# Three products of 12-bit parts in place of seven products of matrix halves, in the projections q, v and g of blocks 2 to 7

## The chip, the cores and the metric

The kernel runs on one core of one Trainium2 chip. The core has five engines with queues of their own: PE (matrix products), DVE (vector work), ACT (activations and copies), POOL (a second, slower vector engine) and SP, which here only issues DMAs. An engine takes its instructions strictly in order, so an instruction that waits holds up all that stand behind it.

The metric is the device time of one execution in microseconds (us), as the median of several runs. A profile is one execution of its own, taken with the hardware profiler. Its span, from the first to the last instruction, is a little shorter than the time of a run.

## The reference

```python
# x: (4, 1024, 512) float32; Wq, Wv, Wo, Wg: (512, 512) float32
x = x + _layernorm(_L0_attn_ref(_layernorm(x), ...))
x = x + _layernorm(_L0_ffn_ref(_layernorm(x), ...))

# _L0_attn_ref
q = (x @ Wq.T).reshape(Bsz, Ls, NHEAD, HEAD_DIM)
v = (x @ Wv.T).reshape(Bsz, Ls, NHEAD, HEAD_DIM)
ret = _retention_scan(v, lam)          # state = lam * state + v_t, along the tokens
out = (q * ret).reshape(Bsz, Ls, D)
out = _layernorm(out, ln_gamma, ln_beta)
g = jax.nn.silu(x @ Wg.T)
return (out * g) @ Wo.T

# _L0_ffn_ref: weights rounded to float8_e4m3, products in float32
gate = jax.nn.silu((x @ gate_w) * gate_scale)
up = (x @ up_w) * up_scale
return ((gate * up) @ down_w) * down_scale
```

Four square products of 512 x 512 (q, v, g, o) and a gated FFN of 512 x 1536 x 512, for 4096 tokens.

## The kernel before

**Blocks and steps.** The tokens are cut into eight blocks of 512 (`t`, lines 1051 on). While block t goes through its FFN in 12 steps (`i`), the next block (`b`) goes through its projections, retention, normalization and output product, and for the one after it (`n`) the input is normalized and turned. All of this is one hand-written order: `pe`, `dve`, `act`, `pool` and `sp` keep each engine's instructions in the order of the code. Each FFN step has eight matmuls for gate (bank `pfg`), eight for up (`pfu`) and eight for down (`pd`, two steps late). Between these groups PE does work for the other blocks.

**FFN.** Activations are split into an upper part and a rest in float32r, a type for which each matmul is written as one instruction; the weights are rounded to few bits already. So each FFN product is two float32r matmuls. `pfg` and `pfu` share two banks (`ps_f`): the next gate needs the bank that ACT's silu of the last gate has read, the next up the bank that DVE's multiplication by the last up (the group `gate<-pfu,us_sb,gate`) has read.

**Square products of blocks 2 to 7.** A float32 matmul is written as two instructions. To need fewer, each 512 x 512 x 512 product is done as seven products of halves instead of eight (a Strassen-Winograd scheme): `product` (line 481) does one, with four matmuls of 256 columns, and DVE and ACT add the seven results together through `mids` (`take`, line 570, hands the finished quarters on: v to the scan, q to the multiplication by the retention, g to silu). The sums of halves that it multiplies are made ahead: those of the weights once, in block 0's steps 8 to 10 (`weight_sums`, line 344, on DVE), and stored in DRAM (`keep_sums`, line 375); those of the input per block (`input_sums`, line 465, four subtractions on POOL into `t_sums`). Products read their weights from `w_ring`, four slots of 256 KB, each refilled by SP after the product that read it (`fetch_weights`, line 384).

**Change of block.** In step 9 x rows 0 and 1 of block b, in steps 10 and 11 rows 2 and 3, get their moments (`st`, `mv`: bn_stats on DVE, power on POOL), are normalized (`x1n`), turned (`xs`/`mxs` by way of DRAM for the first two, `pt` on PE for the last two) and split into `x1nT` by ACT and DVE. The gate matmuls of the next block's step 0 read `x1nT`. In the same steps POOL makes the input sums of block n, and PE does n's first three products of v.

**Block 0.** During block 0's FFN, block 1 is projected with plain float32 matmuls from the whole weights. The FFN weights are rounded during the first steps (`scr`), and in steps 8 to 10 the tiles of wv, wq and wg are turned into sums in place and become `w_ring`, `t_sums` and `mids` from step 9 on.

Of the kernel before, what the change touches and what calls it, by code (L numbers as in the profile page):

```python
# [23 lines left out]
def retention_ffn_sandwich(  # L24
# [286 lines left out]
    def turn_by_blocks(dst, src, tag, name):  # L311
# [21 lines left out]
    order = [("v", j) for j in (1, 2, 6, 7, 4, 5, 3)]  # L333
    order += [("q", j) for j in (1, 6, 2, 7, 4, 5, 3)]
    order += [("g", j) for j in (1, 2, 6, 7, 4, 5, 3)]
    order += [("o", j) for j in (1, 2, 6, 5, 3, 7, 4)]
    banks = {
        "v": {1: 0, 6: 1, 5: 0}, "q": {1: 1, 6: 0, 5: 1},
        "g": {1: 0, 6: 0, 5: 1}, "o": {1: 0, 6: 1, 5: 0},
    }  # L340
    squares = {"v": (wvT, wv_sb), "q": (wqT, wq_sb)}
    operands = {}

    def weight_sums():


        for k, (src, w) in squares.items():
            v = src.rearrange("(c p) f -> p c f", p=P)
            a11, a12, a21, a22 = (w[:, i : i + 2, o : o + H] for o in (0, H) for i in (0, 2))
            operands[k] = {1: v[:, 0:2, 0:H], 2: v[:, 2:4, 0:H], 4: v[:, 2:4, H:D]}  # L350
            made[k] = {5: a22, 7: a21, 6: a11, 3: a12}
            dve.tensor_tensor(a22, a21, a22, ALU.add)
            yield
            dve.tensor_tensor(a21, a11, a21, ALU.subtract)
            yield
            dve.tensor_tensor(a11, a22, a11, ALU.subtract)
            yield
            dve.tensor_tensor(a12, a12, a11, ALU.subtract)
            yield

    made = {}
    adding = weight_sums()

    def output_sums():

        v = woT.rearrange("(c p) f -> p c f", p=P)
        b11, b12, b21, b22 = (wo_sb[:, i : i + 2, o : o + H] for i in (0, 2) for o in (0, H))
        operands["o"] = {1: v[:, 0:2, 0:H], 2: v[:, 2:4, 0:H], 3: v[:, 2:4, H:D]}
        made["o"] = {5: b11, 7: b12, 6: b22, 4: b21}
        dve.tensor_tensor(b11, b12, b11, ALU.subtract)  # L370
        dve.tensor_tensor(b12, b22, b12, ALU.subtract)
        dve.tensor_tensor(b22, b22, b11, ALU.subtract)
        dve.tensor_tensor(b21, b21, b22, ALU.subtract)

    def keep_sums(k):
        for j, t in made[k].items():
            operands[k][j] = dram.tile([P, 2, H], F32, tag=f"sum_{k}{j}", name=f"dsum_{k}{j}", bufs=1)
            sp.dma_start(operands[k][j], t)

    RING = 4  # L380
    total_products = len(order) * (NB - FAST)
    fetched = [0]

    def fetch_weights():
        n = fetched[0]
        if n < total_products:
            k, j = order[n % len(order)]
            sp.dma_start(w_ring[:, n % RING], operands[k][j])
            fetched[0] += 1

    class Retention:


        def __init__(self, t, xt=None):
# [7 lines left out]
            self.made = 0  # L402

# [10 lines left out]
        def new_xnT(self):  # L414
            self.xnT = big.tile([P, TB // Q, NC, Q], F32, tag="xnT", name=f"xnT_{self.t}")
            self.by_chunk = self.xnT.rearrange("p g c j -> p c g j")
# [40 lines left out]
        def fetch_x(self):  # L457
            for a in range(NQ):
                sp.dma_start(
                    self.xnT[ts(a, Q)].rearrange("p g c j -> p g (c j)"),  # L460
# [4 lines left out]
        def input_sums(self, *which, engine=pool):  # L465
            x = self.by_chunk
            b11, b12, b21, b22 = (
                x[:, i : i + 2, g : g + TB // Q // 2, :] for i in (0, 2) for g in (0, TB // Q // 2)
            )
            ts_ = [t_sums[:, k].rearrange("p c (g j) -> p c g j", j=Q) for k in range(4)]  # L470
            self.right = {1: b11, 2: b21, 3: b22, 5: ts_[0], 6: ts_[1], 7: ts_[2], 4: ts_[3]}
            ops = {1: (ts_[0], b12, b11), 2: (ts_[1], b22, ts_[0]), 3: (ts_[2], b22, b12), 4: (ts_[3], b21, ts_[1])}
            for k in which:
                dst, x, y = ops[k]
                engine.tensor_tensor(dst, x, y, ALU.subtract)

        def products(self, n=1):
            for _ in range(n):
                self.product()

        def product(self):

            k, j = order[self.made]
            n = (self.t - FAST) * len(order) + self.made
            self.made += 1
            w = w_ring[:, n % RING]
            if j in (1, 6, 5):
                bank = ps_tile(f"p{k}{j}_{self.t}", f"pa{banks[k][j]}").rearrange("p (c f) -> p c f", c=2)
# [5 lines left out]
            for o in range(2):  # L494
                out_ = bank[:, o]
                if k != "o" and len(self.right[j].shape) == 4:
                    out_ = out_.rearrange("p (g j) -> p g j", j=Q)
                for c in range(2):
                    if k == "o":
                        left, right = self.left[j][:, c, ts(o, P)], w[:, c, :]  # L500
                    else:
                        left, right = w[:, c, ts(o, P)], self.right[j][:, c]
                    pe.matmul(
                        out_, left, right,
# [4 lines left out]
            if k == "o":  # L509
                return self.add_o(j, bank)  # L510
            c12, p1, s167 = (mids[:, m] for m in (1, 2, 3))
# [890 lines left out]
```

## Time and profile before

| what | value |
|---|---|
| runs | 969.64, 970.71, 970.82 us; median 970.71 |
| profiled execution, span | 968.2 us |
| granted TensorE clock | 0.997 |
| DMA | 119.04 MB, mean 123 GB/s |
| float32r matmul, 128x512, gate | 768, mean 400 ns |
| float32 instruction, 128x256, `pq<-t_sums,w_ring` | 192, mean 379 ns |
| two-input operation, DVE, 128x512, `wq_sb<-wq_sb` | mean 684 ns |
| the same on POOL, `x<-x,x1n` | mean 1296 ns |
| waits of PE for others, all named | 5.8 us, the longest 1.9 in two waits for DVE's x1n |

Matmuls are pipelined and their ends are modelled, so the mean of one is longer than the distance of two starts; the rate is read from the starts. Line 74 is that of the helper that keeps the order, so almost every instruction carries it, and groups are told apart by the tiles: `pfu<-x1nT,up_sb` writes `pfu` and reads the other two. A time is counted from the start of the span.

### The profile page before, as it was taken

To read this page: it belongs to the slowest core of one execution; us is meant where nothing else is said; L and a number is where in the kernel's file an instruction comes from. 1 tells how busy PE (TensorE), PEld (TensorE's weight loads), DVE (VectorE), ACT (ScalarE), POOL (GpSimd) and SP (SyncE) were. 2 spreads that over 40 slices of the span, in tenths; PEclk is the share of its full clock that TensorE was granted. 3 is DMA by queue.
4 is the path that set the end of the run, shared out by engine and by line. 5 is a ranking of instruction groups with operands and counts; after the bars stand their busy time and mean duration, and the time that the engine had idled before them with its cause. 6 is when DMAs were issued, how large, how long until landed. Compare 5 with 4: busy or idle time off the path is not lost.

```text
span 968.2 us, 11802 instructions
## 1 busy us (share of the span) xinstructions
PE 955.3 (99%) x4118; PEld 764.9 (79%) x4118; DVE 677.9 (70%) x1038; ACT 406.1 (42%) x637; POOL 283.2 (29%) x356
## 2 busy tenths in 40 slices
PE   9999999999999999999999999999999999999997
PEld 7455767778888888888888888888888888888885
DVE  5996999676768578575685766867667675747445
ACT  3555674468656135331433315332153421524223
POOL 1405121402327042250522415242142512314020
PEclk9999999999999999999999999999999999999998
DMA  9311423762436336463236523364242632314021
GB/s 297 128 53 57 152 66 96 221 217 86 142 97 180 126 91 214 127 191 95 97 109 175 161 80 126 103 171 146 77 152 87 184 121 77 109 44 131 0 88 44
DMA packets 96060, 119.04 MB, mean 123 GB/s; under 512 B 8320, under 2 KB 58240, under 8 KB 96000
## 3 DMA queue, kind: packets, MB, share of 16 engines
q1 hardware_dynamic: 95136, 117.62, 39.6%
q8 instruction: 33, 0.54, 0.2%
q10 hardware_dynamic: 864, 0.66, 0.2%
q14 instruction: 27, 0.22, 0.1%
HBM read 86.00 MB, written 32.24 MB: 122 GB/s over the span
## 4 chain that ended last, share of the span: by engine, by line
PE 87%; DVE 6%; DMA 2%; ACT 2%; POOL 1%; issue 1%; SPq 0%; DVEq 0%; ACTq 0%; POOLq 0%
PE pfg L74 16%; PE pfu L74 16%; PE pd L74 15%; PE pq L74 10%; PE pv L74 10%; PE pg L74 9%; PE po L74 8%; DVE scr L74 1%; DVE st L74 1%; DVE y L74 1%; PE pt L74 1%; DMA xnT<-mx 1%; ACT x1n L74 1%; DVE gate L74 1%; POOL mv L74 1%
## 5 line engine op out<-in xcount | busy, mean ns | idle before, releaser
L74 PE MATMUL pfu<-x1nT,up_sb 128*128 128x512 f32 x768 | 205.1, 409 | 0.0
L74 PE MATMUL pfg<-x1nT,gate_sb 128*128 128x512 f32 x768 | 198.1, 400 | 0.1
L74 PE MATMUL pd<-down_sb,fuse 128*128 128x512 f32 x720 | 189.4, 405 | 0.0
L74 PEld LDWEIGHTS pfu<-x1nT,up_sb 128*128 128x128 f32 x768 | 144.5, 188 | 32.1 <-issue 3.1
L74 PEld LDWEIGHTS pfg<-x1nT,gate_sb 128*128 128x128 f32 x768 | 144.2, 188 | 30.3 <-DVE x1nT L74 0.9
L74 PEld LDWEIGHTS pd<-down_sb,fuse 128*128 128x128 f32 x720 | 135.4, 188 | 27.3
L74 ACT ACTIVATE gate<-pfg,gs_sb 128x512 f32<-128x512 f32 x96 | 65.5, 682 | 169.1 <-PE pfg L74 168.9
L74 ACT CAST fuse<-gate 128x512 fp32r<-128x512 f32 x90 | 55.6, 618 | 176.3 <-DVE gate L74 176.2
L74 DVE SCALAR_TENSOR_TENSOR gate<-pfu,us_sb,gate 128x512 f32<-128x512 f32 x96 | 71.8, 748 | 57.9 <-PE pfu L74 56.5
L74 POOL TENSOR_SCALAR mv<-mv 128x1 f32<-128x1 f32 (+1 forms) x82 | 23.5, 286 | 264.0 <-DVE mv L74 260.8
L74 DVE TENSOR_TENSOR fuse<-gate,fuse 128x512 fp32r<-128x512 f32 x90 | 76.8, 853 | 5.5 <-ACT fuse L74 5.5
L74 POOL TENSOR_TENSOR ysum<-y 128x256 f32<-128x256 f32 (+1 forms) x14 | 14.3, 1024 | 195.7 <-DVE y L74 195.7
L74 DVE BATCH_NORM_STATS2 st<-x 128x6 f32<-128x512 f32 x64 | 43.6, 681 | 29.4 <-POOL x L74 26.2
L74 POOL TENSOR_TENSOR mv<-mv,nhalf 128x1 f32<-128x1 f32 (+1 forms) x75 | 48.6, 649 | 6.2
L74 PE MATMUL pv<-t_sums,w_ring 128*128 128x256 f32 x192 | 45.5, 380 | 0.5 <-POOL t_sums L74 0.5
L74 PE MATMUL pg<-t_sums,w_ring 128*128 128x256 f32 x192 | 45.7, 381 | 0.0
L74 PE MATMUL po<-w_ring,t_sums 128*128 128x256 f32 x192 | 45.4, 379 | 0.0
L74 POOL TENSOR_TENSOR x<-x,x1n 128x512 f32<-128x512 f32 x32 | 41.5, 1296 | 13.2 <-ACT x1n L74 12.8
L74 PE MATMUL pq<-t_sums,w_ring 128*128 128x256 f32 x192 | 45.3, 379 | 0.0
L74 PEld LDWEIGHTS pv<-t_sums,w_ring 128*128 128x128 f32 x192 | 36.1, 190 | 6.6 <-POOL t_sums L74 0.7
L74 PEld LDWEIGHTS pg<-t_sums,w_ring 128*128 128x128 f32 x192 | 35.9, 190 | 6.5 <-ACT mids L74 1.3
L74 PEld LDWEIGHTS po<-w_ring,t_sums 128*128 128x128 f32 x192 | 36.2, 189 | 6.0 <-issue 0.3
(168 smaller groups left out, 1512.5 us busy)
## 6 DMA issues: line engine op xcount, KB each, us to landing
kept<-x SPq DMA_DIRECT2D x32, 256.0 KB, 3.0
x<-kept SPq DMA_DIRECT2D x32, 256.0 KB, 4.1
x<-in_x SPq DMA_DIRECT2D x28, 256.0 KB, 4.3
out<-d SPq DMA_DIRECT2D x27, 256.0 KB, 2.0
xnT<-mx SPq DMA_DIRECT2D x24, 256.0 KB, 4.9
w_ring<-dsum_v SPq DMA_DIRECT2D x24, 256.0 KB, 3.5
w_ring<-dsum_q SPq DMA_DIRECT2D x24, 256.0 KB, 2.6
w_ring<-dsum_g SPq DMA_DIRECT2D x24, 256.0 KB, 2.6
```

What stands on the lines that cost most here:

```text
L74: return lambda *args, **kwargs: tc.keep_in_program_order(op(*args, **kwargs))
```

## The change

In blocks 2 to 7, q, v and g are no longer made of seven products. The input and each weight are split exactly into an upper part of 12 mantissa bits, made by masking off the low 12 bits (`top`), and the rest (`low`). Three float32r passes over the whole 512 columns then go into one bank:

- `a`: the unsplit input times the unsplit weight, which enter by their upper bits,
- `b`: the rest of the input times the scaled rest of the weight, after which ACT rescales the bank in place (PSUM to PSUM),
- `d`: a difference of the input times a difference of the weight, each made of its upper part and its rest.

`begin` does `a`, `b` and the rescaling for 128 output columns, `end` does `d` and hands the bank to the scan, the multiplication or silu. 36 such passes of four matmuls of 512 columns replace 21 products; a table, `gaps`, places them among the FFN's groups, up to three passes in a gap. The product o stays as it was, seven products, with its quarters stored in a new place.

The weights are split in block 0's steps 8 to 10 (`WeightSplit`): masks and differences on DVE, the subtraction on POOL for v and g and on DVE for q, the scaling on ACT. The whole weights are stored in steps 2, 3 and 7, the rests and differences in steps 8 to 10. The input is split per block: `tops_of` (mask on DVE, subtraction on POOL) and `diffs_of` (DVE) for token quarters 0 and 1 in steps 9 and 10, 2 and 3 in steps 10 and 11; for block 2 all in block 0's step 10 and 11. `low` and `diff` take the buffers of wq and wg, `mids` that of wo.

```diff
-    order = [("v", j) for j in (1, 2, 6, 7, 4, 5, 3)]
-    order += [("q", j) for j in (1, 6, 2, 7, 4, 5, 3)]
-    order += [("g", j) for j in (1, 2, 6, 7, 4, 5, 3)]
...
+    LOW = 2.0**-12
+    LOW_MASK = -4096
+    stream = [(k, c, part) for k in "vqg" for c in range(NC) for part in "abd"]
+    stream += [("o", j, None) for j in order_o]
...
+    class WeightSplit:
+        def top(self, h):
+            dve.tensor_scalar(
+                self.tops[h].bitcast(I32), self.half(h).bitcast(I32), LOW_MASK, None, ALU.bitwise_and
+            )
+            self.engine.tensor_tensor(self.half(h), self.half(h), self.tops[h], ALU.subtract)
+        def difference(self, h):
+            dve.scalar_tensor_tensor(self.tops[h], self.tops[h], -LOW, self.half(h), ALU.mult, ALU.add)
+            act.activation(self.half(h), self.half(h), AF.Copy, scale=1.0 / LOW)
...
+    gaps = {
+        -2: [("begin", "v", 0)], -1: [("end", "v", 0), ("begin", "v", 1)],
+        0: [("end", "v", 1)], 1: [("begin", "v", 2)], 2: [("end", "v", 2), ("begin", "v", 3)],
+        3: [("end", "v", 3)], 4: [("begin", "q", 0)], 5: [("end", "q", 0), ("begin", "q", 1)],
...
+    }
...
+        def tops_of(self, *which, engine=pool):
+            if which[0] == 0:
+                self.top = big.tile([P, 4, TB], F32, tag="y", name=f"top_{self.t}")
             for k in which:
-                dst, x, y = ops[k]
-                engine.tensor_tensor(dst, x, y, ALU.subtract)
+                x, top = self.quarter(self.xnT.bitcast(F32), k), self.top[:, k]
+                dve.tensor_scalar(top.bitcast(I32), x.bitcast(I32), LOW_MASK, None, ALU.bitwise_and)
+                engine.tensor_tensor(self.quarter(self.low, k), x, top, ALU.subtract)
+
+        def diffs_of(self, *which):
+            for k in which:
+                low = self.quarter(self.low, k).bitcast(F32)
+                dve.scalar_tensor_tensor(
+                    self.quarter(self.diff, k), low, -1.0 / LOW, self.top[:, k], ALU.mult, ALU.add
+                )
+
+        def pass_of(self, bank, k, c, part, start):
+            w = next_unit(k, c, part).rearrange("p (c f) -> p c f", c=NC)
+            x = {"a": self.xnT, "b": self.low, "d": self.diff}[part].rearrange("p g c j -> p c g j")
+            out_ = bank.rearrange("p (g j) -> p g j", j=Q)
+            for i in range(NC):
+                pe.matmul(
+                    out_, w[:, i, :], x[:, i], start=start and i == 0, stop=True, skip_group_check=True,
+                )
+            fetch_weights()
+
+        def begin(self, k, c, home):
+            bank = self.bank[k, c] = ps_tile(f"p{k}{c}_{self.t}", home)
+            self.pass_of(bank, k, c, "a", True)
+            self.pass_of(bank, k, c, "b", False)
+            act.activation(bank, bank, AF.Copy, scale=1.0 + LOW)
+
+        def end(self, k, c):
+            bank = self.bank.pop((k, c))
+            self.pass_of(bank, k, c, "d", False)
...
-            if t == 0 and 8 <= i < 11:
-                for _ in range(4):
-                    next(adding)
+            if t == 0 and i == 8:
+                tops = scratch(2)
+                split_v = WeightSplit("v", wv_sb, tops[0:2])
+                split_q = WeightSplit("q", wq_sb, tops[2:4], dve)
+                split_v.top(0)
+                split_v.top(1)
+            if t == 0 and i in (9, 10):
+                if i == 9:
+                    split_g = WeightSplit("g", wg_sb, [])
+                split_g.tops.append(work.tile([P, PW], F32, tag="xn", name=f"top_g{i - 9}", bufs=1))
+                split_g.top(i - 9)
             f.gate(i)
...
             if n and i == 11:
-                n.input_sums()
-                n.product()
+                n.diffs_of(2, 3)
+                n.gap(-2)
             f.fuse(i)
+            if t == 0 and i == 8:
+                for h in range(2):
+                    split_v.difference(h)
+                    split_v.keep_difference(h)
+                split_v.keep()
+                split_q.top(0)
+                split_q.top(1)
+            if t == 0 and i in (9, 10):
+                split_g.difference(i - 9)
...
             if fast and i == 9:
...
                 if n:
-                    n.input_sums(1, 2)
+                    n.new_parts()
+                    n.tops_of(0, 1)
...
+            if n and t > 0 and i == 10:
+                n.diffs_of(0, 1)
+                n.tops_of(2, 3)
...
+            if t == 0 and i == 8:
+                for h in range(2):
+                    split_q.difference(h)
+                    split_q.keep_difference(h)
+                split_q.keep()
+            if t == 0 and i in (9, 10):
+                split_g.keep_difference(i - 9)
+                if i == 10:
+                    split_g.keep()
...
             if t == 0 and i == 10:
-                t_sums = wpool.tile([P, 4, 2, H], F32, tag="wq_sb", name="t_sums")
-                mids = wpool.tile([P, 4, 2, H], F32, tag="wg_sb", name="mids")
+                n.new_parts()
+                n.tops_of(0, 1, 2, 3)
+                n.diffs_of(0, 1)
```

## The prediction

> **What bounds the kernel now.** I read the page's busy times and chain first, then PE's order of work at one change of block, then POOL and DVE in the same stretch, then ACT, DVE and SP in the last steps of block 0.
>
> ```profile
> PE 955.3 (99%) x4118; PEld 764.9 (79%) x4118; DVE 677.9 (70%) x1038; ACT 406.1 (42%) x637; POOL 283.2 (29%) x356
> PE 87%; DVE 6%; DMA 2%; ACT 2%; POOL 1%; issue 1%; SPq 0%; DVEq 0%; ACTq 0%; POOLq 0%
> ```
>
> PE works through the whole span. Matmul time taken away comes off the end, and every new PE wait is added to it.
>
> ```profile
> 532.31 1.98 PE L74 MATMUL pfu<-x1nT,up_sb 128*128 128x512 f32 x8
> 534.12 1.98 PE L74 MATMUL pd<-down_sb,fuse 128*128 128x512 f32 x8
> ...
> 539.56 1.89 PE L74 MATMUL pv<-xnT,w_ring 128*128 128x256 f32 x8
> 541.10 2.18 PE L74 MATMUL pd<-down_sb,fuse 128*128 128x512 f32 x8
> 543.12 1.03 PE L74 MATMUL pt<-ident,x1n 128*128 128x128 f32 x8
> 543.99 1.89 PE L74 MATMUL pv<-xnT,w_ring 128*128 128x256 f32 x8
> 545.72 1.89 PE L74 MATMUL pv<-t_sums,w_ring 128*128 128x256 f32 x8
> 547.26 2.18 PE L74 MATMUL pfg<-x1nT,gate_sb 128*128 128x512 f32 x8
> ```
>
> Columns: start, length, what, count. Starts give the rates: eight float32r matmuls of 512 columns take 1.815 us (532.31 to 534.12), 227 ns each. A Strassen product is four matmuls, written as eight instructions; between two float32r groups it takes 1.54 us and lengthens the next group from 1.815 to 2.02, so 1.74 together.
>
> ```profile
> 532.29 1.36 POOL L74 TENSOR_TENSOR t_sums<-xnT,t_sums 128x512 f32<-128x512 f32 x1
> 537.67 1.29 POOL L74 TENSOR_TENSOR x<-x,x1n 128x512 f32<-128x512 f32 x1 [0.18 <-ACT x1n L74]
> 539.04 0.19 POOL L74 TENSOR_SCALAR mv<-mv 128x1 f32<-128x1 f32 x1
> 541.10 1.28 POOL L74 TENSOR_TENSOR t_sums<-xnT 128x512 f32<-128x512 f32 x1
> 539.90 0.55 DVE L74 TENSOR_SCALAR x1n<-x,mv 128x512 f32<-128x512 f32 x1
> 540.37 0.74 DVE L74 SCALAR_TENSOR_TENSOR gate<-pfu,us_sb,gate 128x512 f32<-128x512 f32 x1
> 542.58 1.77 DVE L74 TENSOR_TENSOR fuse<-gate,fuse 128x512 fp32r<-128x512 f32 x1
> 545.49 1.27 DVE L74 TENSOR_TENSOR x1nT<-pt,x1nT 128x512 fp32r<-128x512 f32 x2
> ```
>
> The 99% hides how near DVE is here: from 539.90 it has no gap, and its last x1nT ends at 546.76, 0.50 us before the gate matmul that reads it (547.26). POOL does the small mv operations at once and the two late t_sums after them.
>
> ```profile
> 170.95 0.68 ACT L74 ACTIVATE gate<-pfg,gs_sb 128x512 f32<-128x512 f32 x1
> 173.26 2.84 DVE L74 TENSOR_TENSOR wq_sb<-wq_sb 128x512 f32<-128x512 f32 x4
> 177.69 0.72 DVE L74 SCALAR_TENSOR_TENSOR gate<-pfu,us_sb,gate 128x512 f32<-128x512 f32 x1
> 191.77 2.53 SPq L74 DMA_DIRECT2D dsum_g<-wg_sb  x4
> ```
>
> In block 0 the sums of the weights sit between the operations that free the two pf banks (ACT's silu, DVE's gate), and SP stores them. From 158 to 200 DVE is busy 33.1 of 42.0 us and the DMA engines 76%. (Silu n, gate n, up n and fuse n are those of FFN step n.)
>
> **The change part by part.**
>
> *PE's work.* Each of six blocks loses 21 products, 21 x 1.74 = 36.5, and gets 3 squares x 4 columns x 3 passes x 4 = 144 matmuls x 0.2268 = 32.7. Gain 3.8 a block, **22.7** in all. No row has float32r reading xnT's runs of 32. The nearest: float32 reads them (pq<-xnT, 379 ns) as fast as the contiguous t_sums (379), so I take no cost. Ends: 215 ns (half of the 429 pitch of float32 at 512) gives 33; as far the other way, 239, gives 12.
>
> *Lighter DVE, fuller ACT in steps 0 to 6.* Fifteen additions of 0.685 go, eight scans of 0.72 become four of 1.24; ACT gets nine more PSUM passes of 0.59. The shorter DVE buys nothing: it waited for PE there (25.1 us before mids<-pq). The rescaling of a bank lies under the following eight FFN matmuls (1.8 us). With that cover gone it would cost some 0.8 each, 72 times. It is thin in two places. In block 2 the search (1.57+0.19 each, five a step) stands ahead of it on ACT: I find waits of 0.55, 0.35, 0.3, **1.2** in all. Between mean and variance PE now has 3.65 us of units where it had 5.2 of products, and the variance's second half was 0.9 early: 0.25 a block, **1.5** (0 to 5).
>
> *Ring.* 43 loads of 256 KB a block for 28, still four slots. A slot is refilled when its pass ends, and is read again four units on. The tightest case is the second pass of v3: refilled after v2's first pass, it is read after v2's second pass, eight down matmuls, v2's third and v3's first, 0.91 + 1.82 + 0.91 + 0.91 = 4.5 us later; w_ring's groups land in 2.6 to 3.5. I take 0. At the 5.4 that two of them took under stores (issued at 182) it would be 1 us, twice a step, 12 times a block.
>
> *Change of block, five times.* Before, POOL's late t_sums followed the mv of x rows 2 and 3. Now the four subtractions (1.3 each) go in pairs, the second pair ahead of that mv, and DVE gets four masks (about 0.4, half of 0.68 for 128x1024 int32) and four differences (0.75). Walked on this clock: first masks done 533.3, subtractions until 535.7, mv pair 1.7 and the two x additions (ACT between) until 540.5, second subtractions until 543.15, mv, so x1n at 544.15 for 539.90. Queued behind it on DVE: two differences, gate, x1n, fuse, four x1nT, 6.1 us, so 550.3. PE's own way: the v0 second pass starts 543.25, down 544.15, transpose of row 3 at 547.3, the difference pass and v1's first two until 550.45. Without waits PE would be there at 546.8 (7.70 us from 539.56 before; five passes for three products make it 7.24). **3.6 each, 18.** Ends: 2.0 if masks and differences pass beside POOL, 4.5 if each waits out a POOL operation.
>
> That last pair needs a rule. Row: fuse takes 1.77 while POOL subtracts, 0.68 otherwise; no row has a mask or a two-input scalar_tensor_tensor beside a large POOL operation. The Trainium skill ("SBUF — State Buffer", the practical consequences under who interferes with whom) says that a DVE instruction with two SBUF inputs waits out a GpSimd instruction that reads SBUF, whichever came first keeping the port. By it the differences would pay as fuse does, 4.5 a change of block, and the sum below would end at 997; with none waiting it would end at 985.
>
> *Block 0, steps 8 to 11, once.* It gains six masks of 128x1024 (0.68), four POOL subtractions (2.4, twice 1.28 less overhead), two on DVE (1.22), six differences (1.25, by that 1.22), six ACT scalings (1.15), against twelve additions of 0.69. I walk it in the changed program's order; each time is the end of the thing named. First wait: POOL's two v subtractions 170.2 (they start after the mv of x row 0, 165.4), DVE's v differences 172.6, ACT's v scalings and then x1n of row 1 174.85; DVE's q masks, subtractions, the fuse of step 8 and the q differences 180.5; ACT's q scalings 181.7. Only then ACT comes to silu 9, which began at 170.95 before. PE's gate 10 needs the bank that it frees: 182.4 for 175.91. Second wait: the mask of g's second half reuses the buffer of the first, whose four stores stand on SP behind 24 stores of v and q (0.5 to 0.65 each), a turn's stores, its reload and kept of row 2; they land at 197.5. DVE's gate 10 is queued behind that mask, and up 11, which needs its bank, starts at 199. Third wait: DVE's g difference 202, turn and statistics of row 3 203.5, ACT's x1n 205.7, POOL's addition 207.1 and four low subtractions 212.3; the input differences go into wg's buffer and wait until g's last stores have left it, 214.5; then four differences and a bn_stats 218.2. PE: v0's second pass at 212.4, its third 218.3, transpose 219.6, v1's first two until 221.8, and the next gate at 222.2, behind x1nT, for 197.77. With the 0.46 of this stretch already booked as PE gain, **24.9**. Ends: 18 if every overlap goes well; 34 if the stores, 12,288 more packets of 512 B at 41 ns over 16 engines, 31 us, make the DMA engines the limit.
>
> A second rule bears on these waits. Row: the clock is 1.00 from 4 to 960 us and 0.53 from 963 on, PE having stopped at 961.2. The Trainium skill ("TensorE: Matmul & The Clock Gate", the HAM clock gate) says an idle window of 3.4 us halves the clock until a busy one has passed. By it three waits of block 0 would each cost some 1.7 more, 5 us; I leave them out of the sum, since the chain there runs through other engines.
>
> *Sum.* -22.7 + 1.2 + 1.5 + 18 + 24.9 = **+22.9** on the span of 968.2, so 991. The runs' median, 970.71, lies 2.5 above that span: 970.7 + 22.9 = **993**.
>
> **The rivals.** *PE's gain stands alone*: splits and waits hide as the sums did. 970.7 - 22.7 + 2 = 950, faster. For it: PE had waits of 1.6 us in all at these places before. Against it: only 0.5 us of cover at a change of block, and silu 9 behind twelve new operations. It decides if the walks' losses stay under 22.7. *One of the two losses is hidden*: with block 0's gone 970.7 - 22.7 + 18 + 2.7 = 969; with the five changes of block gone 970.7 - 22.7 + 24.9 + 2.7 = 976. For it: each rests on one engine's order. *The ring starves PE*: 12 us a block on top, 993 + 72 = 1065; against it the 4.5 us. *It isn't one pass per matmul*: float32r at the float32 price, 429 for 227, gives 144 x 0.2 x 6 = 175 more; the FFN's rows exclude that nearly.
>
> **How the numbers follow.** Forecast, slower, 0.76; gain alone 0.13; one loss hidden 0.08; the last two 0.03. From the ends, the forecast's own range is 970.7 - 22.7 + 18 + 10 = 976 to 970.7 - 22.7 + 34 + 22.5 + 5 = 1010, of which I keep up to 1008. To leave no more than 2 in 10 out the range takes in the hidden-loss cases: 966 to 1008. This kernel's measurement tells about 0.2% (2 us) from no change. Faster 0.15 (gain alone and a little of the hidden case), same 0.03, slower 0.82.
>
> **What would show it.** Right: new matmuls at 227 ns; PE idle before pfg and pfu in steps 10 and 11 of block 0, released by ACT gate and DVE gate; some 3 us idle at each change of block, released by POOL low or DVE x1n; PE busy share under 97%. Wrong: a pitch over 235, or idle named after w_ring's loads, or no idle at those places, which would make it 950.

## The result, and the profile after

The changed kernel takes **1017.69 us** (median of 4 runs, 1016.39 to 1019.53), the kernel before 970.50 in the same runs: a ratio of 1.0491, 95% interval 1.0476 to 1.0506. It is slower, as forecast, but by 47 us for the 23 forecast, outside the range of 966 to 1008. The profiled execution has a span of 1015.2 us, 47.0 more than before.

The page of the changed kernel, its busy times and its costliest new group (busy time, mean ns of one, then the idle time ahead of it and who ended that):

```profile
PE 958.3 (94%) x3974; PEld 745.3 (73%) x3974; DVE 635.9 (63%) x984; ACT 443.8 (44%) x697; POOL 298.8 (29%) x344
...
PE 66%; DVE 10%; POOL 8%; DMA 5%; issue 5%; ACT 3%; SPq 2%; DVEq 0%; ACTq 0%; POOLq 0%
...
L74 PE MATMUL pv<-low,w_ring 128*128 128x512 f32 x96 | 30.7, 448 | 24.0 <-POOL low L74 24.0
```

PE's list has 144 matmul instructions fewer and is busy for 3.0 us longer, so the gain is not to be seen even in its busy time; and in the chain that ended last PE's share fell from 87% to 66%, the rest of the way now runs through DVE, POOL and DMA. The list of PE's waits (engine, tile, who ended the wait, us in total, times, longest) of the changed kernel:

```profile
PE pv L74 <- POOL low L74: 24.0, 6, 8.4
PE pfg L74 <- ACT gate L74: 8.4, 2, 5.9
PE pfu L74 <- DVE gate L74: 6.4, 1, 6.4
PE pg L74 <- ACT mids L74: 3.7, 6, 0.6
...
PE pv L74 <- DVE total L74: 1.0, 1, 1.0
PE pv L74 <- DMA w_ring<-unit_v3a: 0.6, 1, 0.6
PE pg L74 <- DMA w_ring<-unit_g3b: 0.6, 1, 0.6
```

Before, all waits came to 5.8 us. The first is one wait per change of block, six of them, 8.4 of it in block 0; the second and third are block 0's; the fourth was not foreseen. Measured from one step's first gate matmul to the next one's, the 47.0 us lie here (the forecast split the same way, from its own terms):

| stretch | measured | forecast |
|---|---|---|
| block 0, twelve steps (103.19 before, 134.42 after) | +31.2 | 24.9 - 0.46 = +24.4 |
| step 11 of blocks 1 to 5, the changes of block | +21.4 | 5 x (3.6 - 0.46) = +15.7 |
| all else of blocks 1 to 6 | -6.0 | -22.7 + 6 x 0.46 + 2.7 = -17.2 |
| ahead of block 0, and block 7 | +0.4 | 0 |
| span | +47.0 | +22.9 |

All three are worse than forecast, by 6.8, 5.7 and 11.2. Two of the forecast's own signs came: PE is busy for under 97% (94%) and idles at the places named. So did one of its signs of being wrong, a pitch (distance of two matmul starts) over 235 ns: the new matmuls start 236 to 237 ns apart (experiment 1). First the change of block, PE's order of work in the changed kernel (start, length, what, count, and the wait ahead of it):

```profile
578.50 1.11 PE L74 MATMUL pv<-xnT,w_ring 128*128 128x512 f32 x4
582.60 2.07 PE L74 MATMUL pv<-low,w_ring 128*128 128x512 f32 x4 [2.99 <-POOL low L74]
584.47 2.66 PE L74 MATMUL pd<-down_sb,fuse 128*128 128x512 f32 x8
...
590.68 1.98 PE L74 MATMUL pfg<-x1nT,gate_sb 128*128 128x512 f32 x8
```

The wait stands where the prediction had it. What follows it was not in the forecast: four matmuls take 1.87 (582.60 to 584.47) where the same four elsewhere take 0.95, and eight of down 2.50 for 1.82. The busy times of those stretches (PE, PEld, DVE, ACT, POOL, then the granted clock, DMA share, GB/s) say why:

```profile
582.60:584.50 1.90, 1.90 (x5) 1.51 (x6) 1.01 (x2) 0.00 (x0) 1.57 (x4) 0.50 0.02 6
584.50:586.00 1.50, 1.50 (x5) 1.21 (x4) 1.50 (x4) 0.65 (x2) 0.00 (x0) 0.54 0.12 27
586.00:587.00 1.00, 1.00 (x6) 0.73 (x6) 0.95 (x2) 1.00 (x3) 0.00 (x0) 1.00 0.69 221
```

The clock was 0.50 to 0.54 for 3.4 us after the wait, then 1.00. In block 0, PE of the changed kernel:

```profile
182.16 3.78 PE L74 MATMUL pfg<-x1nT,gate_sb 128*128 128x512 f32 x8 [5.87 <-ACT gate L74]
...
195.89 3.07 PE L74 MATMUL pfg<-x1nT,gate_sb 128*128 128x512 f32 x8 [2.50 <-ACT gate L74]
205.33 3.78 PE L74 MATMUL pfu<-x1nT,up_sb 128*128 128x512 f32 x8 [6.37 <-DVE gate L74]
...
219.09 2.07 PE L74 MATMUL pv<-low,w_ring 128*128 128x512 f32 x4 [8.40 <-POOL low L74]
...
230.23 1.88 PE L74 MATMUL pfg<-x1nT,gate_sb 128*128 128x512 f32 x7 [0.57 <-DVE x1nT L74]
```

Gate 10 starts at 182.16, forecast 182.4. From there on things are late: a wait of 2.5 before gate 11 that was not forecast at all, up 11 at 205.3 for 199, the next block's gate at 229.3 (its later matmuls at 230.2) for 222.2. Who held up ACT and DVE, from their own order of work:

```profile
191.87 0.62 ACT L74 CAST x1nT<-x1n 128x512 fp32r<-128x512 f32 x1 [8.18 <-DMA unit_q3d<-scr]
...
203.92 0.69 DVE L74 TENSOR_SCALAR top_g<-wg_sb 128x1024 int32<-128x1024 int32 x1 [6.36 <-DMA unit_g3d<-top_g]
...
222.40 1.29 DVE L74 SCALAR_TENSOR_TENSOR diff<-low,top 128x512 fp32r<-128x512 f32 x2 [10.08 <-DMA unit_g3b<-wg_sb]
```

All three wait for stores. The second and the third are those of the prediction, which had the third end at 214.5; x row 3's moments stand behind it on DVE, and with them the next block's gate. The first is the surprise: block 1's `x1nT` takes the buffer in which the splits of v and q lay (`scr`), so ACT's cast of row 0 cannot start before the last store of q's differences has left it, and ACT's silu of step 10 is queued behind that cast.

### The profile page after: what moved, and what is told of

Same layout as the page of the kernel before. It is cut to its first block, busy times and chain, and to the rows that moved or that the text cites. A ratio compares the mean times of both kernels' runs of the same rounds, so it can differ in the third digit from the quotient of the medians.

```text
span 1015.2 us, 11825 instructions
## 1 busy us (share of the span) xinstructions
PE 958.3 (94%) x3974; PEld 745.3 (73%) x3974; DVE 635.9 (63%) x984; ACT 443.8 (44%) x697; POOL 298.8 (29%) x344
## 4 chain that ended last, share of the span: by engine, by line
PE 66%; DVE 10%; POOL 8%; DMA 5%; issue 5%; ACT 3%; SPq 2%; DVEq 0%; ACTq 0%; POOLq 0%
PE pd L74 12%; PE pfg L74 12%; PE pfu L74 11%; PE pv L74 9%; PE po L74 8%; PE pq L74 8%; PE pg L74 7%; POOL low L74 2%; SPq L74 2%; DVE st L74 2%; POOL mv L74 2%; DVE scr L74 1%; DVE y L74 1%; DVE gate L74 1%; DVE fuse L74 1%
## 5 line engine op out<-in xcount | busy, mean ns | idle before, releaser
L74 PE MATMUL pfu<-x1nT,up_sb 128*128 128x512 f32 x768 | 198.5, 401 | 6.4 <-DVE gate L74 6.4
L74 POOL TENSOR_SCALAR mv<-mv 128x1 f32<-128x1 f32 (+1 forms) x82 | 27.7, 338 | 264.2 <-DVE mv L74 260.3
L74 DVE TENSOR_TENSOR fuse<-gate,fuse 128x512 fp32r<-128x512 f32 x90 | 78.3, 870 | 10.2 <-ACT fuse L74 10.2
L74 POOL TENSOR_TENSOR ysum<-y 128x512 f32<-128x512 f32 x8 | 11.0, 1369 | 214.3 <-DVE y L74 214.3
L74 POOL TENSOR_TENSOR mv<-mv,nhalf 128x1 f32<-128x1 f32 (+1 forms) x75 | 54.3, 725 | 6.2
L74 PE MATMUL pv<-low,w_ring 128*128 128x512 f32 x96 | 30.7, 448 | 24.0 <-POOL low L74 24.0
L74 DVE TENSOR_TENSOR y<-pq,y 128x512 f32<-128x512 f32 x24 | 16.6, 692 | 54.7 <-PE pq L74 54.7
L74 POOL TENSOR_TENSOR d<-d,x 128x512 f32<-128x512 f32 x28 | 36.0, 1310 | 22.7 <-ACT d L74 20.9
L74 ACT ACTIVATE pv<-pv 128x512 f32<-128x512 f32 x24 | 14.0, 582 | 65.1 <-PE pv L74 65.1
L74 PEld LDWEIGHTS pv<-low,w_ring 128*128 128x128 f32 x96 | 19.3, 207 | 31.2 <-POOL low L74 26.8
L74 DVE RECIPROCAL rstd<-rstd 128x512 f32<-128x512 f32 x8 | 26.8, 3352 | 21.8 <-ACT rstd L74 21.8
```

The costliest lines, as they stand in the source:

```text
L74: return lambda *args, **kwargs: tc.keep_in_program_order(op(*args, **kwargs))
```

## The experiments

Times are medians of four runs; the changed kernel is 1017.69 (1016.39 to 1019.53), and the kernel before, measured again beside the experiments, stayed between 970.5 and 971.3. The runs of one kernel spread over 1 to 5 us.

**1. Reading contiguous columns.** Tokens and channels of the input are mixed up by this edit.

```diff
-            x = {...}[part].rearrange("p g c j -> p c g j")
-            out_ = bank.rearrange("p (g j) -> p g j", j=Q)
+            x = {...}[part].rearrange("p g c j -> p (g c j)")
+            x = x.rearrange("p (c f) -> p c f", c=NC)
+            out_ = bank
```

> Every matmul of q, v and g in blocks 2 to 7 reads 512 columns that lie side by side in place of sixteen runs of 32 (the tokens and channels are mixed up by it, so q, v and g are not those of the reference; count and shape of the matmuls stay). The changed kernel's new matmuls start 236 to 237 ns apart, those of the FFN 227. Theory (the strided reading costs 10 ns a matmul): pitch 227 in all three passes, 864 x 0.0098 = 8.5 us shorter, 1009. Rival (the ring's weights, or the bank that is added to, cost it): pitch stays 237, 1017 to 1018.

**1008.53**, 9.2 less. PE's order of work, first in the changed kernel, then in this one, each between the same three groups:

```profile
595.26 1.11 PE L74 MATMUL pv<-xnT,w_ring 128*128 128x512 f32 x4
596.21 1.11 PE L74 MATMUL pv<-low,w_ring 128*128 128x512 f32 x4
597.15 1.98 PE L74 MATMUL pd<-down_sb,fuse 128*128 128x512 f32 x8
```

```profile
591.55 1.07 PE L74 MATMUL pv<-xnT,w_ring 128*128 128x512 f32 x4
592.46 1.07 PE L74 MATMUL pv<-low,w_ring 128*128 128x512 f32 x4
593.37 1.98 PE L74 MATMUL pd<-down_sb,fuse 128*128 128x512 f32 x8
```

Four matmuls take 0.945 from start to start when each reads sixteen runs of 32, 0.91 when the columns lie side by side: 236 and 227 ns. The length in the second column blurs this (1.11 and 1.07 contain the modelled end); starts show it. The theory holds, and the rival (the ring's weights, or adding to the bank) falls. One thing went with the reading: the bank, which lies side by side in both kernels, is no longer described as sixteen runs of 32. Experiment 7 changes both together too, so no run parts the two. The prediction's count of PE's work comes out once the columns are contiguous: in this kernel block 6, the last one with new matmuls and without a split of the input at its end, is 2.8 us shorter than before, 3.4 without its wait for ACT's mids, where the count gives 3.8 - 0.46 = 3.3.

**2. Work in the wait.**

```diff
-            self.pass_of(bank, k, c, "a", True)
+            again = 0 if (k, c) != ("v", 0) else 8 if self.t == FAST else 3
+            self.pass_of(bank, k, c, "a", True, again)
...
-            for i in range(NC):
+            for i in list(range(NC)) * (1 + again):
```

> v0's first pass is repeated in the wait before its second one: three times more in blocks 3 to 7 (2.8 us of the 3.0 to 3.5 us), eight times more in block 2 (7.6 of 8.4 us); each repetition starts its sum anew, so the result is the same. Theory (the wait makes the clock fall to half, and that costs 0.9 in v0's second pass and 0.7 in the down group after it): both run at 237 and 227 ns, and each change of block is 1.1 to 1.4 shorter, until DVE's last x1nT (589.6 for a gate that starts at 590.7) sets the end; 5.5 to 7 in all, nothing in block 0, where DVE's differences set the next pass: 1011. Rival (the clock falls on its own, whatever PE does): 1017 to 1018, the slow matmuls stay.

**1014.30**, 3.4 less, so more work for PE made the kernel faster. Busy times and clock over v0's second pass and the down group behind it, in this kernel:

```profile
584.60:585.84 1.24, 1.05 (x4) 0.86 (x5) 0.16 (x1) 0.00 (x0) 0.99 (x4) 1.00 0.29 40
585.84:587.70 1.86, 1.86 (x10) 1.49 (x9) 1.86 (x4) 0.58 (x1) 0.72 (x2) 1.00 0.62 175
```

The clock stays at 1.00, the four matmuls take 1.05, the eight 1.83. What step 11 has over the kernel before fell in four of the five changes (5.10 to 3.60, 4.48 to 3.60, 4.56 to 3.59, 3.62 to 2.65) and not in the first (3.62 to 3.68), 4.3 together, under the 5.5 to 7 expected. The exception fits: in the changed kernel PE waited 2.98 to 3.52 us at each change, and after the first wait (3.07) its four matmuls took 1.05, the clock 1.00.

So the length of a wait does not decide: 3.07 left the clock alone and 2.98 halved it. The trace of the changed kernel shows what went with it. Its granted clock changes only at times that lie a whole number of steps of 3.41 us apart. Here are five such stretches and, last, the half-speed one behind the fifth (columns as above; the value behind the comma is PE's busy time):

```profile
193.34:196.75 3.41, 0.91 (x5) 0.73 (x5) 1.10 (x3) 2.37 (x5) 1.28 (x1) 1.00 0.87 227
336.70:340.11 3.41, 1.63 (x8) 0.97 (x6) 1.75 (x4) 3.38 (x5) 3.27 (x4) 1.00 0.31 117
340.12:343.53 3.41, 2.13 (x9) 1.76 (x10) 1.25 (x3) 0.66 (x2) 2.78 (x6) 1.00 0.36 112
459.58:462.99 3.41, 0.50 (x2) 0.45 (x3) 0.88 (x2) 0.17 (x1) 3.24 (x5) 1.00 0.65 217
579.05:582.46 3.41, 0.56 (x3) 0.11 (x1) 1.42 (x4) 0.80 (x2) 3.41 (x3) 1.00 0.62 214
582.46:585.87 3.41, 3.27 (x8) 2.59 (x9) 2.38 (x5) 0.58 (x1) 1.65 (x5) 0.50 0.06 20
```

The first wait (3.07) lies across a boundary: PE is busy for 1.63 and 2.13 of its two stretches, and the clock stays. In the other four changes one stretch holds nearly the whole wait (PE busy for 0.42 to 0.56), and the clock is at one half for the next one. In block 0 a stretch with a wait of only 2.50 (busy 0.91) was enough. All thirteen traces agree: away from their start and end, every such stretch at full clock in which PE was idle for more than 0.55 of the time was followed by half speed, and none with less than 0.37 was. The Trainium skill ("TensorE: Matmul & The Clock Gate", the HAM clock gate) has a window of about 3.4 us that runs freely, and this trace agrees with both; it asks for an idle window, though, where here one that was idle for 2.5 of its 3.4 us was enough.

**3. POOL's late subtractions behind mv.**

```diff
-        -2: [("begin", "v", 0)], -1: [("end", "v", 0), ("begin", "v", 1)],
-        0: [("end", "v", 1)], ...
+        -2: [("first", "v", 0), ("first", "v", 1)], -1: [("second", "v", 0), ("second", "v", 1)],
+        0: [("end", "v", 0), ("end", "v", 1)], ...
             if n and t > 0 and i == 10:
                 n.diffs_of(0, 1)
-                n.tops_of(2, 3)
             if fast and i == 10:
                 b.x1_moments(2)
                 b.x1_moments(3)
                 b.x1n_of(2)
+            if n and t > 0 and i == 10:
+                n.tops_of(2, 3)
```

`first` is the first pass, `second` the second with the rescaling; `n.diffs_of(2, 3)` moves behind the last `rest_of(3)` of step 11.

> At the change of block POOL's subtractions for token quarters 2 and 3 come after the mv of x rows 2 and 3, DVE's differences of these quarters after the four x1nT, and PE does the first passes of v0 and v1 first, both second passes after the transposes, both difference passes after the next gate. Theory (the order on POOL, low ahead of mv, is the whole loss at the change): on the clock of the change at 578 us mv starts at 580.1 for 582.6, x1n of row 3 is ready at 582.0 to 582.6, low at 584.6 under the down group, next gate 586.7 for 590.7, no halved clock: 4 each, 20 in all, 998, and 1 to 3 more in block 0. Rival (DVE's own work, masks and differences, sets it): x1nT comes out at the same time, at most 5 in all, 1012.

**1009.98**, 7.7 less. Step 11 got 16.7 shorter over the five changes; but one pass per change (0.95) has only moved into the next step 0, which the expectation forgot, and step 0 grew by up to 2.1. DVE and POOL at one change of this kernel:

```profile
581.16 2.68 POOL L74 TENSOR_TENSOR low<-xnT,top 128x512 fp32r<-128x512 f32 x2
...
581.70 1.02 DVE L74 TENSOR_SCALAR x1n<-x,mv 128x512 f32<-128x512 f32 x1
582.64 1.75 DVE L74 TENSOR_TENSOR fuse<-gate,fuse 128x512 fp32r<-128x512 f32 x1
584.32 1.28 DVE L74 TENSOR_TENSOR x1nT<-x1n,x1nT 128x512 fp32r<-128x512 f32 x2
```

At this change no wait of PE is over 1 us any more, and the clock stays at 1.00. What is left is DVE: with POOL's subtractions now beside its last operations, x1n takes 1.02 for 0.55 and fuse 1.75 for 0.68. So the order on POOL was about half of the loss. The other half goes with the two engines working beside each other, which experiment 8 takes apart.

**4 and 5. Block 0 in parts.** In the fourth kernel the rests and differences of the weights are made but not stored, in the fifth not made either (`top` and `difference` are empty).

```diff
-            keep_units(self.k, "b", by_unit(self.w))
+            for c in range(NC):
+                operands[self.k, c, "b"] = operands[self.k, c, "a"]
...
-                sp.dma_start(operands[self.k, c, "d"][:, 2 * h : 2 * h + 2, :], d[:, :, ts(c, P)])
+                operands[self.k, c, "d"] = operands[self.k, c, "a"]
```

> The splits of the weights are made, but the rests and differences are not stored: the second and third passes read the unsplit weights (their products are not those of the reference). 36 stores of 512 B packets on SP go. Theory (the stores hold up block 0: the mask of g's second half, up 11 behind it, and x1nT, which takes the buffer of q's differences): the wait of 6.4 us before up 11 and the one of 2.5 before gate 11 go, the input's low starts 8 to 10 earlier: 1006 to 1009. Rival (the splits themselves, on DVE, ACT and POOL, fill the stretch): the waits before gate 10 (5.9) stays in both; here up 11 stays late too, at most 2 gained, 1015.

> The weights are neither split nor stored in parts: second and third passes read the unsplit weights (their products are not those of the reference). Of block 0's additions only the input's masks, subtractions and differences are left. Theory (the splits' operations and their stores make block 0's loss): without the stores alone 12 of 31 us went in the profile; without the operations the wait before gate 10 (5.9) goes too and low of the input, 8 to 10 late in step 11, comes in its turn: block 0 loses 4 to 6, 990 to 993. Rival (what is left, the input's four subtractions on POOL behind the x of row 3, sets the end of step 11 by itself): over 12 stays, 998 or more.

**1002.16** without the stores, 15.5 less; **996.02** without the splits, 21.7 less. In the profiles block 0 loses 19.1 and 8.0 in place of 31.2. By the medians the stores were the larger part and more than expected; by the profiles the two steps weigh about the same, 12.1 and 11.1. The waits before gate 11 and up 11 are gone with them, that before gate 10 (5.9) stays, as both theories had it, and goes in the fifth. What remains without any split, 8.0, lies between the 4 to 6 of the theory and the rival's 12. PE and DVE of the fifth kernel:

```profile
198.74 2.08 PE L74 MATMUL pv<-low,w_ring 128*128 128x512 f32 x4 [8.83 <-POOL low L74]
...
194.16 3.40 DVE L74 SCALAR_TENSOR_TENSOR diff<-low,top 128x512 fp32r<-128x512 f32 x2 [3.10 <-POOL low L74]
```

It is the change of block once more: POOL's four subtractions stand ahead of the mv of x row 3, as the rival had it, though they cost less than it said. The second line also prices what no row of before showed: a difference with two SBUF inputs beside POOL's subtraction takes 1.7 (3.40 for two), alone 0.68.

**6. Silu 9 ahead of the scalings, fewer stores.**

```diff
+            if t == 0 and i == 9:
+                split_q.scale(0)
+                split_q.scale(1)
+                split_q.keep()
```

These lines stand behind `f.gate(9)`; `difference` no longer scales q, and each half of a difference is stored by two DMAs.

> The two ACT scalings of q's rests and their stores come after silu 9 in place of before it, and a difference's half is stored with two DMAs in place of four (24 stores for 36). Theory (order on ACT and the stores cost, not the amount of work): silu 9 at 174.5, the wait before gate 10 falls from 5.9 to under 1; the buffers that wait for stores (x1nT's, that of the mask of g's second half) come free 4 to 6 earlier: 10 to 12 less, 1006 to 1008. Rival (DVE is full from step 8 to 11, 43 us of work in 42, whatever the order): gate 10 is early, but the 6 us come back before up 11 or in step 11: 1014 to 1017.

**1017.26**: nothing gained. PE's wait before gate 10 (5.9) is gone, and 4.4 stand before up 10, 4.3 before gate 11 (2.5 in the changed kernel) and 7.2 before up 11 (6.4). ACT in this kernel:

```profile
190.87 0.62 ACT L74 CAST x1nT<-x1n 128x512 fp32r<-128x512 f32 x1 [7.97 <-DMA unit_qd<-scr]
```

The cast waits as long as before, for the same bytes in half as many DMAs. Its stores of 256 KB in 512 B packets land some 0.9 us apart (v's rests at 183.6, 184.6, 185.5 and 186.4), those of 128 KB in the changed kernel 0.46 apart (q's differences at 190.2, 190.7, 191.2, 191.6): here the bytes ahead in the queue set the time, not the number of issues. The rival is right in its outcome, but not in its reason: DVE idles 5.8 us at that place.

**7. Rests and differences side by side, and g's banks.**

```diff
-            shape = [P, TB // Q, NC, Q]
+            shape = [P, NC, TB]
...
-                elif (k, c) in (("g", 1), ("g", 2)):
-                    self.begin(k, c, "pa0")
+                elif k == "g":
+                    self.begin(k, c, f"pa{(0, 1, 1, 0)[c]}")
...
-            var = ps_tile(f"var_{self.t}", "pa1" if self.fast else "pa")
+            var = ps_tile(f"var_{self.t}", "pa0" if self.fast else "pa")
```

> The rests and differences of the input are made channel chunk by channel chunk and written with 512 tokens side by side, so the second and third passes read contiguous columns and only the first one runs of 32; and g's banks and that of the variance change places (g1, g2 on pa1, g3 and the variance on pa0), so that g1 does not wait for the silu of g0. Theory: pitch 227 in 576 matmuls, 0.0098 x 576 = 5.6 us, and the six waits for ACT's mids (0.6 each, 3.7) go: 9.3 together, 1008. Rival: writing or reading in runs makes POOL's and DVE's operations longer than 1.28 and 0.68, and the change of block gives 5 or more back, 1013 or more; or the wait at g1 comes back at g2 or at the variance, then 1012.

**1007.48**, 10.2 less, 9.3 expected. The six waits for ACT's mids are gone from PE's list; the variance waits 1.4 in all for DVE's half in their place. POOL's subtractions stayed at 1.3 with runs of 32 as their source.

**8. All subtractions of the input in step 9.**

```diff
                 b.x1_moments(0)
                 b.x1_moments(1)
+                if n:
+                    n.new_parts()
+                    n.tops_of(0, 1, 2, 3)
```

> As the run with low after mv, but in blocks 1 to 5 all four masks and subtractions of the input follow the moments of x rows 0 and 1 in step 9, where POOL is idle until 573 on the clock of the change at 577. Theory (x1n of row 3 and the fuse, 1.02 and 1.75 long beside POOL's low, are what was left of the loss): both fall to 0.55 and 0.7, the next gate at 584.9 for 586.35, 1.4 at each of five changes: 7 less than with low after mv, 1003. Rival (the same waits of DVE for POOL only move to step 9 and 10, to its x1n, fuse and moments, and DVE has not enough slack there): no gain over that run, 1010 or more.

**1024.32**, 14 more than experiment 3 and slower than the changed kernel itself. DVE, then PE, of this kernel:

```profile
575.04 3.59 DVE L74 TENSOR_SCALAR top<-xnT 128x512 int32<-128x512 int32 x4 [1.17 <-DMA xnT<-mx]
578.55 0.74 DVE L74 SCALAR_TENSOR_TENSOR gate<-pfu,us_sb,gate 128x512 f32<-128x512 f32 x1
...
579.34 3.15 PE L74 MATMUL pfu<-x1nT,up_sb 128*128 128x512 f32 x8 [2.42 <-DVE gate L74]
```

The masks come to DVE before their data has landed and wait 1.17; four of them then take 3.59, for 1.42 where POOL is idle, since POOL's subtractions run beside the last two (1.5 each, 0.42 for the first two). Queued behind them is the gate operation that frees up 10's bank, and PE waits 2.4 for it; step 10 is 2.9 to 6.6 longer than before the change at the five changes. Step 11 itself got 1.2 shorter than before the change, so the reading of experiment 3 was right and the place was wrong: the rival's outcome.

**9. Only the order of the stores.**

```diff
                     split_v.keep_difference(h)
-                split_v.keep()
...
                 split_g.difference(i - 9)
+                split_g.keep_difference(i - 9)
+                if i == 9:
+                    split_v.keep()
+                    split_q.keep()
```

`split_q.keep()` and g's `keep_difference` leave their old places.

> Only SP's order in block 0's steps 8 and 9 is changed: the stores of the differences of v, q and of g's first half come before those of the rests of v and q, and no longer behind x row 2's copy and the ring's first loads. Same operations, same bytes. Theory (two buffers wait for stores: x1nT takes that of q's differences, whose last store lands at 190.8, and g's second mask that of the first, landing at 203.6): the cast of x1nT row 0 at 188 for 191.9, the wait before gate 11 (2.5) gone; the second mask at 193 to 195 for 203.9, the wait before up 11 (6.4) down to 2 or less; 8 to 10 less, 1008. Rival (the amount of work on DVE, ACT and POOL sets the end of step 11 and the stores only hide behind it): the waits move to POOL's low, 1015 to 1018.

**1010.36**, 7.3 less, block 0 at +25.9. ACT, then PE, of this kernel:

```profile
187.94 0.62 ACT L74 CAST x1nT<-x1n 128x512 fp32r<-128x512 f32 x1 [4.69 <-DMA unit_q3d<-scr]
...
196.48 2.12 PE L74 MATMUL pfu<-x1nT,up_sb 128*128 128x512 f32 x8 [2.21 <-DVE gate L74]
204.08 2.05 PE L74 MATMUL pv<-xnT,w_ring 128*128 128x512 f32 x4 [5.48 <-DMA w_ring<-unit_v0a]
210.30 2.07 PE L74 MATMUL pv<-low,w_ring 128*128 128x512 f32 x4 [4.18 <-POOL low L74]
```

The cast comes at 187.9 (188 expected), gate 11 has no wait, up 11 waits 2.2 for 6.4. The theory holds. It left out a wait of 5.5: the ring takes wv's buffer, so its first load now stands behind v's and q's rests. That wait costs little, since the pass behind it has to wait for POOL's low until 210.3, and POOL's chain to it does not use the ring. What sets the end is the third hand-over: DVE's differences of the input wait 11.6 for the last store of g's rests, until 215.1, for 222.4 in the changed kernel.

**10 and 11. All orders together, and without the splits.** The edits of 3, 6 (ACT), 7 and 9, and in block 0 the input's masks and subtractions behind the moments of x row 3, its differences behind the `x1nT`. The eleventh adds that of experiment 5.

> All reorderings together, exact results: low after mv at every change (in block 0 the input's masks and POOL's subtractions come after the moments of x row 3 too, the differences after the x1nT), rests and differences side by side, g's banks, q's scalings behind silu 9, the order of stores. Theory (the losses are separate and add up): 1017.7 less 7.7 (low after mv), 10.2 (side by side and banks), 8 to 10 (stores and silu 9), 4 to 5 (row 3 in block 0): 985 to 988. Rival (block 0 is full: DVE has 43 us of work in 42 us of steps 8 to 11): block 0 gives under 5, 993 to 1000. Faster than the kernel before (971) by neither.

> As all orders together, but the weights are neither split nor stored in parts (second and third passes read the unsplit weights, the products are not those of the reference): what the three passes are worth in blocks 2 to 7 when block 0 costs nearly nothing. Theory (losses add up): 996.0 less 7.7, 10.2 and 4 to 5 = 973 to 975; against 971 before the gain of PE, 22.7 by my count less 3 for the runs of 32 that are left, is then still eaten by some 20 us of waits at the changes and in step 0 after them. Rival (with block 0 free the passes win): 960 or less.

**986.99** (ratio to before 1.0175, interval 1.0159 to 1.0191) and **975.15** (1.0050, 1.0032 to 1.0068): the first inside what the separate losses add up to, the second at its upper end. PE's waits in the tenth:

```profile
PE pfu L74 <- DVE gate L74: 7.1, 2, 4.4
PE pv L74 <- DMA w_ring<-unit_v0a: 5.5, 1, 5.5
PE pt L74 <- DVE x1n L74: 5.3, 5, 1.3
PE pfg L74 <- DVE x1nT L74: 5.1, 5, 1.0
```

The first two are block 0's, which still loses 16.2 of the 16.9 that this profile is above that of before; the others are DVE's x1n and x1nT at the changes. Two thirds of the loss (30.7 of 47.2) were order and layout. Even with no split of the weights at all (and so with the wrong products), the three passes only come to within half a per cent of the kernel before: no version tried here beats it.

## Why the prediction was right on the side and wrong on the size

Three terms of the sum missed by much: PE's gain was put some 8 us too high, the changes of block 5.7 and block 0 6.8 too low. Smaller terms missed both ways.

**PE's work.** "I take no cost" for reading runs of 32 was the step that cost most. It was argued from a row of another type. The pitch is 236 to 237 ns, almost the upper end of 239 that the prediction had set and did not use. So 144 matmuls take 34.07 us a block and the gain is 36.5 - 34.07 = 2.43, 14.6 in all for 22.7; experiment 1 measured the difference at 9.2. Some 7.3 of it (744 of the 864 matmuls) lie in the third row of the table and make up most of its 11.2; waits for ACT's mids, the ring and a sum of the search (5.9 in all, for 2.7 booked) make up 3.2. The estimate had looked for the cost in a float32 row (379 and 379 ns), where it did not show; there a column takes about twice as long (216 ns for 256 columns, 227 for 512 in float32r).

**The range.** Its upper end was added up with the full 22.7 of gain. With the gain of 12 that belongs to 239 ns, it would have ended at 970.7 - 12 + 34 + 22.5 + 5 = 1020, and held. The bound was worked out and then left out of the sum. It would have held by luck in part: the other ends in it, 4.5 a change of block if the differences waited for POOL, 34 in block 0 if the DMA engines were the limit, 5 for the variance, stand for causes that did not come.

**The lighter DVE, the fuller ACT.** The 1.2 for the search (ACT's passes `seen` over the FFN weights) and 1.5 for the variance did not come where they were put: no wait of PE is named after a rescaling or the variance. One wait of 1.0 belongs to the search in another place, where v's first pass waits for DVE to read the search's last sum (`total`) out of a bank. ACT did cost 3.7, at a place not looked at: g1 begins in the bank that g0's silu still reads, and that silu stands behind the squares and the step's own silu. Experiment 7 took it away by other banks.

**The ring.** 0 was near: two waits of 0.6.

**Change of block.** Place, order and the engine named (POOL's low ahead of mv) were right, and PE waited 2.98 to 3.52 where the walk had about 3. Measured +21.4 for +15.7: 4.3 of the difference is the halved clock (experiment 2), 1.0 the pitch of five passes each. The prediction had the clock's rule before it and applied it to block 0 alone, and there left it out of the sum; as quoted it asks for an idle window of 3.4 us, which a wait of 3 is not, and the stretches under experiment 2 show that less was enough. That DVE's differences would wait out POOL did not happen in this order: they ran at 0.68 beside mv. Where they meet a subtraction they pay 1.7 (experiment 5), as the rule of the Trainium skill quoted there says ("SBUF — State Buffer", the practical consequences under who interferes with whom).

**Block 0.** The walk was exact to its first wait, and in its steps too (POOL's v subtractions 170.5 for 170.2, DVE's q differences 180.4 for 180.5, gate 10 182.16 for 182.4). It then missed the buffer that `x1nT` takes over from the splits, which put 8.2 us of waiting into ACT's queue, and what follows came some 6 to 7 later. Experiment 9 shows that the order of the stores did it: with another order, block 0 is back to +25.9. Its points lie near those of the walk: up 11 at 196.5 for 199, the second pass at 210.3 for 212.4, the differences' wait over at 215.1 for 214.5, the next gate at 223.4 for 222.2. The new order moved the stores that `x1nT` waits for together with those that the second mask waits for, so how much each of the two cost is not shown. The clock, left out of the sum there, was at one half for 30.7 us of this stretch in the changed kernel; no run shows what that cost by itself. This stretch is also the one that varies: the kernels above that leave its splits and stores as they are had 31.2 to 35.1 in their profiles, so a difference of a few us there rests on the medians, and 25.9 lies well outside.

**The rivals.** The gain alone, or one loss hidden, is excluded: both losses stand in the waits. The ring (1.2 in all) and the float32 price (429 ns a matmul for the measured 237) did not come, as expected.

## What to carry to other kernels

When an upper bound has been worked out for one term, put it into the range, above all if the same text argues that the cheap value has no row of its own. Before costing work on an idle engine, list every buffer that the new tiles take over and the next tiles take over from them: here taking away the stores, with three such hand-overs behind them (two of them forecast), gained 15.5 us, and taking away the operations as well 6.2 more. And where PE is to wait for about 3 us, as here, count the halved clock after it as possible, or give PE something harmless to do meanwhile.

## What was not expected of the hardware

A float32r matmul of 512 columns started every 227 ns with contiguous columns and every 236 to 237 with sixteen runs of 32 (128 B each). After four of five waits of 2.98 to 3.52 us the granted clock fell to 0.5 for 3.41 us, and it went not by the wait's length but by how much of it lay in one 3.41 us step of the clock (experiment 2). A mask with one SBUF input (0.42 alone) took 1.5 beside POOL's subtraction, and an x1n 1.02 for 0.55: not only operations with two inputs pay. The profile of before had this already, 1.27 us behind the x1n of 0.55 that the prediction quotes, while POOL makes its t_sums:

```profile
541.17 1.50 DVE L74 TENSOR_SCALAR x1n<-x,mv 128x512 f32<-128x512 f32 x1
```

The prediction said that no row has a mask beside a large POOL operation; this row, of the same operation with one SBUF input, was the nearest one.
